# First half of the first layer's W2 from a split operand, two lower parts by accumulating DMAs, and the last store whole on one queue

## The chip, the core and the metric

The kernel runs on one core of one Trainium2 chip. The metric is the device time of one execution in microseconds. A core has a matrix engine (PE, with its weight loads shown as PEld), a vector engine (DVE), a scalar engine (ACT), a general engine (POOL) and a queue engine (SP); each takes its own instructions in program order and waits on semaphores for the others. SP and ACT issue DMAs; in the changed kernel POOL issues two as well.

## The reference

Two layers follow each other on x of shape 4 x 512 x 256, all in float32. Each layer takes a layer norm `xn` of x, a mixer `s` of it, and a feed-forward `g`, and sets `x = x + s * silu(g)`.

- Mixer of layer 0: a recurrence that starts from a zero state, so that only its input part is left: `y = sum over 16 of (C_real*B_real - C_imag*B_imag) * (xn @ W_in.T)`, then `y @ W_out.T`, an RMS norm with weight `norm_w`, and the residual `xn`.
- Mixer of layer 1: a second layer norm with gamma and beta, causal attention with one head of 256, an output projection, and the residual.
- Feed-forward of both layers: `hidden = silu(xn @ W1.T) * (xn @ W3.T)` with 1024 columns, a Walsh-Hadamard transform of `hidden` along the 1024, and `hidden @ W2.T` back to 256 columns.

## The kernel before

**Split operands.** Most float32 operands of PE are kept as a pair of type fp32r: `hi` is the value rounded to fp32r, `lo` is the value less `hi`. A product of two pairs is three products, hi·hi, hi·lo and lo·hi. `split(src, hi, lo)` (L59) makes a pair with two instructions: `nc.scalar.copy` on ACT (L61) rounds, and a `tensor_tensor` subtract on DVE (L62) gives the rest.

**Folded weights.** The Hadamard transform is put into W2 (`prep_w2`, L143): for each half of the 256 output columns, three rounds of adds and subtracts on DVE (`w2b`, L155 and L156) transform across the eight blocks of 128 rows, and a product with the 128 x 128 Sylvester matrix transforms within a block. The result `w2ps` goes through `split` into `w2h` and `w2l`. For the first half of layer 0 the product takes the float32 matrix `had_f` and the float32 `cur` as they are (`native`); for the other three halves `cur` is split into `w2bh` and `w2bl` and multiplied with the fp32r matrix `had` in two products. W_in, W_out and the B, C sums are folded into one 256 x 256 matrix `m` (`prep_m`, L191): `wgh`, `wgl` are W_out scaled by `g`, `wih`, `wil` are W_in split, and `mps` is their product.

**The up weights** `w13` of layer 0 come in four quarters of 512 KB (`load_w13`), each split into hi and lo when the feed-forward first needs it (`split_w13`, L122). They are held in SBUF and used for all four batches.

**Order.** The batch loop runs the feed-forward `ffn` of layer 0 for one batch at a time. For each of its eight column chunks c it emits six products for the gate (`gu` j = 0) and six for the linear part (j = 1), silu on ACT (L527), the gate multiply on DVE (L528), a split of the hidden chunk, and the down products `dn`. The products of `gu` go to three rotating PSUM banks, so that a bank must have been read by silu or by the gate multiply before the third next product can begin. Between the chunks, `Beside` hands out steps of other tasks. In batch 0 the tasks are `prep_first` (L965: the W2 of layer 0, `prep_m`, the load of the next x) and the mixer. A scheduler with a timing model then decides the order on each engine within these dependencies; `after(ins)` asks that what follows is placed behind `ins`. The task steps therefore do not alone decide the order: an engine's order in the built program does. Scratch tiles of `w2b` for layer 0 lie in the slots of later x tiles (`x_slot`), so the loads of x 1 to 3 wait for them.

**The end.** In layer 1 `gate_tile` (L1058) ends the last batch in four tiles of 128 rows: silu on ACT (L1061), multiply (L1063) and add (L1064) on DVE, and a store. Each add is placed behind the one before by `first["last"]`. Tiles 0 to 2 are stored whole (128 KB) by SP; tile 3 is stored as two halves of 64 rows, one by SP, one by ACT.

Of the kernel before, what the change touches and what calls it, by code (L numbers as in the profile page):

```python
# [11 lines left out]
F32 = mybir.dt.float32  # L12
# [3 lines left out]
F32R = mybir.dt.float32r  # L16
# [19 lines left out]
def kernel(ctx: ExitStack, tc: tile.TileContext, a: dict, out: bass.AP):  # L36
# [22 lines left out]
    def split(src, hi, lo, engine=nc.vector):  # L59

        h = nc.scalar.copy(hi, src)  # L61
        return h, engine.tensor_tensor(lo, src, hi.bitcast(F32), ALU.subtract)  # L62

    line = {"fixed": False, "last": None}
# [55 lines left out]
    def split_w13(layer, q, raw):  # L122
        both = wp.tile([P, 2, 2, S], F32R, tag="w13", name=f"w13_{layer}_{q}", bufs=4)
        hi, lo = both[:, 0], both[:, 1]
        if (layer, q) != (0, 0):
            split(raw, hi, lo)
            return hi, lo
        halves = [slice(c * D, (c + 1) * D) for c in range(2)]
        split(*(z[:, :, halves[0]] for z in (raw, hi, lo)))
        next(normed)  # L130
        with after(first["norm"][0]), after(first["norm"][1]):
            hi_, lo_ = split(*(z[:, :, halves[1]] for z in (raw, hi, lo)))
        first["w13"] = hi_, lo_
        return hi, lo
# [8 lines left out]
    def prep_w2(layer, raws, dst, scratch):  # L143

        w2h, w2l = dst
        for half in range(2):
            ds_ = slice(half * P, (half + 1) * P)
            cur = raws[half]  # L150
            for st, h in enumerate((1, 2, 4)):
                nxt = scratch(f"w2b{st}_{layer}_{half}", [P, NH, P])
                cv = cur.rearrange("p (g two h) d -> p g two (h d)", two=2, h=h)
                nv = nxt.rearrange("p (g two h) d -> p g two (h d)", two=2, h=h)
                nc.vector.tensor_tensor(nv[:, :, 0], cv[:, :, 0], cv[:, :, 1], ALU.add)  # L155
                nc.vector.tensor_tensor(nv[:, :, 1], cv[:, :, 0], cv[:, :, 1], ALU.subtract)  # L156
                cur = nxt
                yield

            native = layer == 0 and half == 0  # L160
            if not native:
                bh = t4(f"w2bh_{layer}_{half}", [P, NH, P], F32R)
                bl = t4(f"w2bl_{layer}_{half}", [P, NH, P], F32R)
                split(cur, bh, bl)
                yield
            for q in range(2):
                o = psum(f"w2ps_{layer}_{half}_{q}", [P, NH // 2, P])
                qs = slice(q * NH // 2, (q + 1) * NH // 2)
                if native:
                    matmul(o, had_f, cur[:, qs, :], start=True, stop=True)  # L170
                else:
                    matmul(o, had, bh[:, qs, :], start=True, stop=False)
                    matmul(o, had, bl[:, qs, :], start=False, stop=True)
                split(o, w2h[:, qs, ds_], w2l[:, qs, ds_])
                yield

# [11 lines left out]
        nc.sync.dma_start(win, a["w_in"].rearrange("(c p) i -> p c i", p=P))  # L188
        return win, wout

    def prep_m(win, wout):  # L191

        cb = wp.tile([P, 4, 2, DS], F32, name="cb")
        nc.vector.tensor_tensor(cb, bc[:, :, 0:2, :], bc[:, :, 2:4, :], ALU.mult)
        cbd = wp.tile([P, 4, DS], F32, name="cbd")
        nc.vector.tensor_tensor(cbd, cb[:, :, 0, :], cb[:, :, 1, :], ALU.subtract)
        g = wp.tile([P, 4], F32, name="g")
        nc.vector.tensor_reduce(g, cbd, AX.X, ALU.add)
        wg = [t4(f"wg{i}", [P, 4, D], F32R) for i in "hl"]
        wi = [t4(f"wi{i}", [P, 4, D], F32R) for i in "hl"]  # L200
        for c in range(4):
            nc.scalar.mul(wg[0][:, c, :], wout[:, c, :], g[:, c : c + 1])
            nc.vector.scalar_tensor_tensor(
                wg[1][:, c, :], wout[:, c, :], g[:, c : c + 1], wg[0][:, c, :].bitcast(F32),
                ALU.mult, ALU.subtract,
            )
        split(win, *wi)
        yield
        hi, lo = (wp.tile([P, 2, D], F32R, name=f"m{i}") for i in "hl")
        o = psum("mps", [P, 2, D])  # L210
        for i in range(2):
            mm3(
                o[:, i, :],
                [(tuple(z[:, k, sl(i)] for z in wi), tuple(z[:, k, :] for z in wg)) for k in range(4)],
            )
        split(o, hi, lo)
        first["m"] = hi, lo
        yield
# [247 lines left out]
    def ffn(name, xT, w13, w2, slot, defer=1, spare=(), parts=1, behind=False, tail=()):  # L466
# [34 lines left out]
        for c in range(NH):  # L501
            with after(gates[-2] if behind and c >= 2 else None):
                wh, wl = w13(c // 2)
            gu = []
            for j in range(2):

                o = psum(f"{name}gu{c}_{j}", [P, S], **(DN[0] if behind and c == 1 else GU))
                cols = slice((c % 2) * D + j * P, (c % 2) * D + (j + 1) * P)
                gu.append((o, cols))
            for half in range(parts if c == 0 else 1):  # L510
                n = S // (parts if c == 0 else 1)
                ts_ = slice(half * n, (half + 1) * n)
                if parts == 1 or c:
                    for o, cols in gu:
                        last_up = mm3(o[:, ts_], k_pairs((wh, wl), cols, xT, ts_))
                    continue

                for n, (w, x) in enumerate(((wh, xT[0]), (wl, xT[0]), (wh, xT[1]))):
                    for o, cols in gu:
                        for k in range(2):  # L520
                            last_up = matmul(
                                o[:, ts_], w[:, k, cols], x[:, k, ts_],
                                start=n + k == 0, stop=n + k == 3,
                            )
            gu = [o for o, _ in gu]
            h = hid(f"{name}h{c}")
            first["silu"] = nc.scalar.activation(h, gu[0], AF.Silu)  # L527
            gates.append(nc.vector.tensor_tensor(h, h, gu[1], ALU.mult))  # L528
            first["gate"] = gates[-1]
            if c < len(spare):  # L530
                hh, hl = spare[c]
            else:
                hh = hid(f"{name}hh{c}", F32R)
                hl = hid(f"{name}hl{c}", F32R)
            if c < len(spare):
                nc.scalar.copy(hh, h)
                late.append((hl, h, hh))
            else:
                split(h, hh, hl)
            for _ in range(2 if c >= NH - 2 else 0):  # L540
                if late:
                    lo_, h_, hi_ = late.pop(0)
                    with after(gates[-1]):
                        nc.vector.tensor_tensor(lo_, h_, hi_.bitcast(F32), ALU.subtract)
            queue.append((c, hh, hl))
            ups = last_up if behind else None
            with after(gates[-1] if behind else None), after(ups):
                slot(2 * c)
            if len(queue) > defer:
                down(*queue.pop(0))  # L550
            with after(gates[-1] if behind else None), after(ups):
                slot(2 * c + 1)
# [412 lines left out]
    def prep_first():  # L965
        steps = prep_w2(0, raw2, w2, x_slot)
        with after(first["w13"][1]):
            next(steps)
        yield
        for _ in range(4):  # L970
            next(steps)
            yield
        with after(first["silu"]):
            nc.scalar.copy(had, had_f)
        for _ in range(2):
            next(steps)
            yield
        for _ in range(2):
            next(steps)
            yield  # L980
        load_x(1)
        product = prep_m(*raw_m)
        next(product)
        yield
        next(steps)
        yield
        next(product)
        yield
        yield from steps
# [15 lines left out]
    for b in range(B):  # L1005
        tasks = []
        if b == 0:
            prep = prep_first()
            next(prep)
            tasks.append((prep, 12))  # L1010
        if b:
            tasks.append((call(gate_all, f"g0_{b - 1}", dn, xns[0, b - 1], xs[b - 1]), 1))
        tasks.append((mixer(b), MIXER))
# [44 lines left out]
    def gate_tile(t, o):  # L1058
        x, s = xs[B - 1][:, t, :], xns[1, B - 1][:, t, :]
        g = t2(f"gl{t}", [P, D])  # L1060
        nc.scalar.activation(g, o, AF.Silu)  # L1061
        with after(first.get("last")):
            nc.vector.tensor_tensor(g, g, s, ALU.mult)  # L1063
        first["last"] = nc.vector.tensor_tensor(x, x, g, ALU.add)  # L1064
        if t + 1 < NT:
            nc.sync.dma_start(out[B - 1, sl(t), :], x)
            return

        for queue, rows in ((nc.sync, slice(0, P // 2)), (nc.scalar, slice(P // 2, P))):
            queue.dma_start(out[B - 1, sl(t), :][rows], x[rows])  # L1070

    loaded = {}

# [127 lines left out]
```

## Time and profile before

| what | value |
|---|---|
| median of 3 runs | 359.46 us (359.22 to 359.85) |
| the profiled execution | 359.25 us |
| its span, first to last instruction | 357.5 us |
| PE busy | 350.7 us, 98% of the span |
| DVE busy | 287.2 us, 80% |
| ACT busy | 197.5 us, 55% |
| POOL busy | 20.8 us, 6% |
| granted PE clock | 0.998 |
| DMA | 52.25 MB, mean 146 GB/s |

1.8 us of the execution lie outside the span. Shares of the whole span hide stages: the kernel has a start of some 8 us in which the inputs arrive, a long middle, and an end of some 5 us. The lines of a timeline give start, duration, engine, source line, operation, output <- inputs, shapes and a count of merged instructions; where a line merges several, the time to the next line's start says more than the duration, because products overlap their neighbours. DVE and ACT instructions overlap a little too: a 128x512 subtract shows 0.68 us, and the next starts 0.60 us after it.

### The profile page before, as it was taken

The page shows a single profiled execution, that of the slowest core. Times are in us where ns is not written, and L with a number is a line of the kernel's source. Part 1 is how long each engine was busy: PE and PEld are TensorE (multiplying, and loading weights), DVE is VectorE, ACT ScalarE, POOL GpSimd, SP SyncE. Part 2 cuts the span into 40 slices and gives each one's busy share as a digit, 9 for nine tenths or more (in the row PEclk, how much of TensorE's full clock was granted, in tenths as well). Part 3 has the DMA queues.
Part 4 walks back from the last instruction along what each step waited for, and adds up shares of the span by engine and source line. Part 5 has one row for each costly group of instructions (what it writes and reads, how often), then busy time and mean ns, then how long its engine had stood idle before and what let it go on. Part 6 is the DMA issues. An engine that isn't in the chain of part 4 may idle for free.

```text
span 357.5 us, 6276 instructions
## 1 busy us (share of the span) xinstructions
PE 350.7 (98%) x2477; PEld 326.8 (91%) x2477; DVE 287.2 (80%) x597; ACT 197.5 (55%) x373; POOL 20.8 (6%) x22
## 2 busy tenths in 40 slices
PE   7999999999999999999999999999999999999994
PEld 5878998888988898888999999999999999999994
DVE  6899659998579938998887957989679897577645
ACT  4666166265463425674467745586455676555443
POOL 2000110300021110100100001100011000000000
PEclk9999999999999999999999999999999999999999
DMA  7935000301054316756257135662554635444401
GB/s 241 337 87 211 2 1 2 117 0 61 0 169 174 131 42 230 257 179 200 96 210 261 54 153 208 229 234 73 201 208 172 217 145 205 176 146 173 185 0 59
DMA packets 16300, 52.25 MB, mean 146 GB/s; under 512 B 1648, under 2 KB 7952, under 8 KB 16272
## 3 DMA queue, kind: packets, MB, share of 16 engines
q1 hardware_dynamic: 15904, 51.54, 40.9%
q8 instruction: 19, 0.31, 0.4%
q10 hardware_dynamic: 368, 0.33, 0.3%
q14 instruction: 9, 0.07, 0.1%
HBM read 42.40 MB, written 9.45 MB: 145 GB/s over the span
## 4 chain that ended last, share of the span: by engine, by line
PE 95%; DVE 3%; DMA 1%; ACT 0%; issue 0%; DVEq 0%
PE f_0dn L70 6%; PE f_1dn L70 6%; PE f_2dn L70 6%; PE f_0gu L70 6%; PE f_1gu L70 6%; PE f_2gu L70 6%; PE f_3gu L70 6%; PE f_3dn L70 5%; PE sc L70 4%; PE pv L70 4%; PE o L70 3%; PE v L70 3%; PE tq L70 3%; PE w2ps L70 1%; PE pt L70 1%; PE mps L70 1%
## 5 line engine op out<-in xcount | busy, mean ns | idle before, releaser
L70 PE MATMUL f_3gu<-xt,w 128*128 128x512 f32 x96 | 25.0, 396 | 0.0
L70 PE MATMUL f_2gu<-xt,w 128*128 128x512 f32 x96 | 24.8, 395 | 0.0
L70 PE MATMUL f_1gu<-xt,w 128*128 128x512 f32 x96 | 24.8, 395 | 0.0
L70 PE MATMUL f_0gu<-xt,w 128*128 128x512 f32 (+1 forms) x108 | 24.3, 378 | 0.0
L70 PEld LDWEIGHTS f_0gu<-xt,w 128*128 128x128 f32 x108 | 18.4, 188 | 4.6 <-issue 0.7
L70 PEld LDWEIGHTS f_1gu<-xt,w 128*128 128x128 f32 x96 | 17.0, 188 | 3.1
L70 PEld LDWEIGHTS f_2gu<-xt,w 128*128 128x128 f32 x96 | 17.0, 188 | 3.0
L70 PEld LDWEIGHTS f_3gu<-xt,w 128*128 128x128 f32 x96 | 17.0, 188 | 2.9
L61 ACT CAST f_2hh<-f_2h 128x512 fp32r<-128x512 f32 x16 | 10.0, 622 | 15.5 <-DVE f_2h L528 12.4
L70 PE MATMUL f_3dn<-w2l,f_3hh 128*128 128x256 f32 x64 | 17.7, 281 | 0.0
L70 PE MATMUL f_3dn<-w2h,f_3hh 128*128 128x256 f32 x64 | 17.7, 281 | 0.0
L70 PE MATMUL f_1dn<-w2l,f_1hh 128*128 128x256 f32 x64 | 17.7, 281 | 0.0
L70 PE MATMUL f_2dn<-w2h,f_2hh 128*128 128x256 f32 x64 | 17.7, 282 | 0.0
L70 PE MATMUL f_1dn<-w2h,f_1hh 128*128 128x256 f32 x64 | 17.6, 280 | 0.0
L70 PE MATMUL f_2dn<-w2l,f_2hh 128*128 128x256 f32 x64 | 17.6, 281 | 0.0
L70 PE MATMUL f_3dn<-w2h,f_3hl 128*128 128x256 f32 x64 | 17.0, 281 | 0.0
L70 PE MATMUL f_1dn<-w2h,f_1hl 128*128 128x256 f32 x64 | 17.0, 281 | 0.0
L70 PE MATMUL f_2dn<-w2h,f_2hl 128*128 128x256 f32 x64 | 16.7, 281 | 0.0
L61 ACT CAST f_3hh<-f_3h 128x512 fp32r<-128x512 f32 (+1 forms) x17 | 10.0, 594 | 10.1 <-DVE f_3h L528 5.9
L61 ACT CAST f_1hh<-f_1h 128x512 fp32r<-128x512 f32 x16 | 9.9, 622 | 9.7 <-DVE f_1h L528 6.6
L62 DVE TENSOR_TENSOR f_2hl<-f_2h,f_2hh 128x512 fp32r<-128x512 f32 x16 | 10.9, 684 | 4.5 <-ACT f_2hh L61 4.5
L62 DVE TENSOR_TENSOR f_3hl<-f_3h,f_3hh 128x512 fp32r<-128x512 f32 (+1 forms) x17 | 11.0, 654 | 3.7 <-ACT f_3hh L61 3.6
(487 smaller groups left out, 1145.9 us busy)
## 6 DMA issues: line engine op xcount, KB each, us to landing
sw<-s SPq DMA_DIRECT2D x32, 896.0 KB, 5.2
s<-sp SPq DMA_DIRECT2D x8, 512.0 KB, 4.3
s<-sp SPq DMA_DIRECT2D x8, 384.0 KB, 2.8
w2raw<-in_w SPq DMA_DIRECT2D x4, 512.0 KB, 5.6
sraw<-in_w SPq DMA_DIRECT2D x4, 512.0 KB, 3.6
mrb<-there SPq DMA_DIRECT2D x4, 512.0 KB, 3.7
w13raw<-in_w SPq DMA_DIRECT2D x3, 512.0 KB, 7.1
x<-in_x SPq DMA_DIRECT2D x3, 512.0 KB, 3.6
```

Source lines behind the costliest of these rows:

```text
L61: h = nc.scalar.copy(hi, src)
L62: return h, engine.tensor_tensor(lo, src, hi.bitcast(F32), ALU.subtract)
L70: ins = call(*args, **kwargs)
```

## The change

- In `prep_w2` the `native` path goes: the first half of layer 0 is split into `w2bh` and `w2bl` and multiplied with `had` in two products per quarter, as the other three halves are.
- A new helper `split_by_dma` makes a pair without DVE: ACT writes `-src`, rounded to fp32r, into `lo`; ACT copies `src` rounded into `hi`; and POOL issues a DMA that adds `src` onto `lo`. Quarter 3 of the up weights and W_in are made this way. The former is placed behind the third silu of batch 0.
- The split of W_in moves from `prep_m` into `prep_first`, before the second half of W2, and `prep_first` is counted as 13 steps instead of 12.
- In `gate_tile` the last tile is stored whole by SP, and only the adds of tiles 2 and 3 are entered in `first["last"]`.

```diff
+    def split_by_dma(src, hi, lo):
+        nc.scalar.mul(lo, src, -1.0)
+        nc.scalar.copy(hi, src)
+        nc.gpsimd.dma_start(lo.bitcast(F32), src, accum_op=ALU.add)
...
-        if (layer, q) != (0, 0):
-            split(raw, hi, lo)
+        if q:
+            with after(first["silus"][2] if q == 3 else None):
+                (split_by_dma if q == 3 else split)(raw, hi, lo)
             return hi, lo
...
-            native = layer == 0 and half == 0
-            if not native:
-                bh = t4(f"w2bh_{layer}_{half}", [P, NH, P], F32R)
-                bl = t4(f"w2bl_{layer}_{half}", [P, NH, P], F32R)
-                split(cur, bh, bl)
-                yield
+            bh = t4(f"w2bh_{layer}_{half}", [P, NH, P], F32R)
+            bl = t4(f"w2bl_{layer}_{half}", [P, NH, P], F32R)
+            split(cur, bh, bl)
+            yield
...
-                if native:
-                    matmul(o, had_f, cur[:, qs, :], start=True, stop=True)
-                else:
-                    matmul(o, had, bh[:, qs, :], start=True, stop=False)
-                    matmul(o, had, bl[:, qs, :], start=False, stop=True)
+                matmul(o, had, bh[:, qs, :], start=True, stop=False)
+                matmul(o, had, bl[:, qs, :], start=False, stop=True)
...
-    def prep_m(win, wout):
+    def prep_m(wi, wout):
...
-        wi = [t4(f"wi{i}", [P, 4, D], F32R) for i in "hl"]
...
-        split(win, *wi)
...
             first["silu"] = nc.scalar.activation(h, gu[0], AF.Silu)
+            first.setdefault("silus", []).append(first["silu"])
...
-        for _ in range(4):
+        for _ in range(3):
             next(steps)
             yield
         with after(first["silu"]):
             nc.scalar.copy(had, had_f)
         for _ in range(2):
             next(steps)
             yield
-        for _ in range(2):
+        win, wout = raw_m
+        wi = [t4(f"wi{i}", [P, 4, D], F32R) for i in "hl"]
+        split_by_dma(win, *wi)
+        for _ in range(4):
             next(steps)
             yield
         load_x(1)
-        product = prep_m(*raw_m)
+        product = prep_m(wi, wout)
...
-            tasks.append((prep, 12))
+            tasks.append((prep, 13))
...
-        first["last"] = nc.vector.tensor_tensor(x, x, g, ALU.add)
-        if t + 1 < NT:
-            nc.sync.dma_start(out[B - 1, sl(t), :], x)
-            return
-
-        for queue, rows in ((nc.sync, slice(0, P // 2)), (nc.scalar, slice(P // 2, P))):
-            queue.dma_start(out[B - 1, sl(t), :][rows], x[rows])
+        ins = nc.vector.tensor_tensor(x, x, g, ALU.add)
+        if t > 1:
+            first["last"] = ins
+        nc.sync.dma_start(out[B - 1, sl(t), :], x)
```

## The prediction

> **What bounds the kernel now.** I read the page first, then the chain of waits, then the stretches in which the change lies, engine by engine.
>
> ```profile
> PE 350.7 (98%) x2477; PEld 326.8 (91%) x2477; DVE 287.2 (80%) x597; ACT 197.5 (55%) x373; POOL 20.8 (6%) x22
> PE 95%; DVE 3%; DMA 1%; ACT 0%; issue 0%; DVEq 0%
> 20.00:31.00 11.00, 11.00 (x47) 8.54 (x46) 11.00 (x21) 7.51 (x14) 0.00 (x0) 1.00 0.49 147
> 51.00:75.00 24.00, 24.00 (x140) 20.91 (x140) 23.11 (x47) 11.06 (x25) 3.42 (x2) 1.00 0.13 44
> ```
>
> The second line is the chain by engine; the last two are windows (length, then PE, PEld, DVE, ACT, POOL busy, clock, DMA share, GB/s). From 8 to 352 us PE is the path without a hole, at the full clock. So a product saved there is time saved, and a wait put there is time lost. DVE is as full as PE in 20 to 31 us and nearly so in 51 to 75, so its order decides whether PE's banks come free in time. Next, the chain in order of time (start, length, what), for the products that change:
>
> ```profile
> 17.87 0.86 PE w2ps L70 x2
> 18.73 1.40 PE f_0gu L70 x6
> 20.13 0.86 PE w2ps L70 x2
> 27.29 0.23 PE w2ps L70
> ```
>
> One native float32 product takes PE 0.86 us, one product of the split kind 0.23, and six up products 1.40. Then the end, from the timelines of DVE, SP and ACT (start, length):
>
> ```profile
> 353.89 0.42 DVE L1064 TENSOR_TENSOR x<-x,gl 128x256 f32<-128x256 f32 x1
> 354.34 0.55 SPq L1070 DMA_DIRECT2D out<-x  x1
> 354.35 0.57 ACTq L1070 DMA_DIRECT2D out<-x  x1
> out<-x SPq DMA_DIRECT2D x1, 64.0 KB, 2.0
> out<-x ACTq DMA_DIRECT2D x1, 64.0 KB, 2.3
> ```
>
> The last two, from the DMA view, say how long the halves take to land; after the later one 0.8 us of closing waits remain to 357.5.
>
> **The change part by part.**
>
> W2's first half. Two native products (2 x 0.86) become four split ones (4 x 0.23): 0.80 us less on PE, all on the path. The new split costs ACT one 1024-wide copy (1.05 us) and DVE one 1024-wide subtract, from which the next instruction starts 1.14 later.
>
> The two lower parts. DVE loses two 1.14 us subtracts (rows of w13's last quarter, 25.33, and of `wil`, 30.51). ACT gains two 1024-wide multiplies; the trace has none, so I take its 512-wide activation and cast (0.59 and 0.62) as equal and give each the 1024 cast's 1.05, starting the next 0.95 later. Both copies move earlier.
>
> The waits that this makes, walked along the new orders of the engines with row durations, and 0.05 us from one engine's end to another's start. To 17.71 nothing changes for PE.
> - ACT: the third silu needs the second `early` copy, which needs the gate multiply that ends at 16.13, so silu runs at 16.69, the multiply for `lo` at 17.18, its copy at 18.12, and the new `w2bh` only at 19.06, to 20.11. PE has done six up products by 19.11 and three more by 19.81, and its next are the two `w2bh` products: a wait of 0.35.
> - DVE: the third gate begins at 17.32; then the first `w2b` pair of the second half to 19.12, w13's third quarter to 20.26, the next pair to 21.46, the new `w2bl` to 22.60, and the fourth gate ends at 23.28. PE arrives at the chunk that needs that bank at 23.20 and goes on at 23.33: a wait of 0.13.
> - From there I find no late partner until the up products of batch 0 are done: gates at 25.28 and 29.09 against PE at 26.13 and 30.34, `w2bh` of the second half at 25.98 against 27.53. PE reaches the point that was at 36.06 at 35.74.
> - So 0.80 - 0.48 = 0.32 us are left. The cover of these waits is ACT's spare time; with ACT free earlier they would be nothing, and with each ACT step 0.1 us longer the first would be 0.6.
>
> Batch 1's order moves too: DVE does the whole first `w2b` chain before the second gate. The first gate starts 4.12 us after batch 1's first product (when its silu is done). Up to the fourth gate DVE has six `w2b` pairs (12 x 0.60), three gates and three lower parts (6 x 0.60), the norm's statistics (1.78), `w2bl` (1.13), the scaled mixer rows (1.59) and the residual (1.13): 16.43. With the gate's own 0.68 and the handover it is done at 21.28 after that first product, and PE wants the bank at 21.16. A wait of 0.12; the sum is good to about 0.3, so the bounds are nothing and 0.5. Net so far 0.20. Everything behind has DVE holes in the trace before, and I put it at nothing, within 0.3 either way.
>
> The adding DMAs. Neither a DMA issued by POOL nor an accumulating one is in the trace. Nearest rows: 512 KB loads land 3.1 us (`qkraw`) to 8.9 us (w13's last quarter, in the crowded start) after issue; the x loads, alone, 3.6; 896 KB takes 5.2. An add reads its target as well, so about 1 MB of reads, and on from 3.6 and 5.2 that is some 5.7: my value, since the DMA engines idle at 19 to 21.5 us; bounds 3.1 to 8.9. The first is issued at 18.2, and PE, which would stand before three waiting products, wants it at 26.8: 8.6 us of cover. The second is issued at 22.1, beside the loads of x 1 and 2, and is wanted at 31.9: 9.8 us. So both cost nothing by the value, 0.3 by the upper end. The scale of W_out on DVE also waits for the first (slot), at 28.9. Behind them on POOL stands the power of batch 1's norm at 40, long after. The x loads on SP keep their releases (the second half's `w2b` at 21.5, 24.7, 27.9) within 0.1.
>
> POOL's own work shows a price beside a full DVE: the same 128x4 power takes 1.01 us at 40.66 and 1.91 at 64.71. If POOL's part in a DMA is stretched alike, that is inside my bounds. The Trainium skill, SBUF — State Buffer, "Summary: rules for kernel authors", speaks against the change: it says not to hide a POOL-issued DMA under DVE work, because its descriptors starve; "Who interferes with whom" limits that to DVE's two-port modes, which it says `tensor_tensor`, all that DVE runs at 18 to 24 us, does not have. By the strict rule the first add would start only when DVE runs dry, some us after PE stops at 26.8, and the sum would turn to a loss of several us, an estimate; by the limit it is as above. DMA: Bandwidth & Descriptors, "Anatomy of one DMA", gives 2.0 us plus bytes at 436 GB/s, an estimate of 3.2 us for a plain 512 KB; by it the sum stays.
>
> The end. Each add no longer follows the one before for tiles 0 and 1, so DVE runs gl, gl, x, x without a dependent pair: the last add ends 0.08 earlier (pairs show 0.45, independent ones 0.35). The halves land at 356.36 and 356.64, 2.0 and 2.3 after issue. The trace's landing counts put the three whole 128 KB stores just before at 1.70 to 1.72 after theirs. The fourth, issued in the same rhythm, I give 1.70: 0.60 less. Bounds: 1.70, and 2.29 if the halves' lateness has nothing to do with being two.
>
> **Sum.** 0.20 + 0.08 + 0.60 = 0.88 us. The profiled execution has 359.25, so 358.37; it lies 0.21 below the median of the runs, to which this belongs: 358.6.
>
> **The rivals.**
> 1. The adding DMA is late. POOL prepares it slowly beside a full DVE, or the add runs far below a copy's rate. PE stands at the second three products of chunk 6; each us beyond 8.6 is 1 us lost. The gain is gone at 9.5 us and it is measurably slower from 10.2. At 11 us: 358.6 + 2.4 = 361.0. For it: no row to hold it back, and the 1.91 us power. Against: idle DMA engines, and twice the loads' 3.6 is still in time.
> 2. The gain is eaten by waits: ACT's four 1024-wide steps in a row, or batch 1's DVE order, cost 0.6 more than walked, or the whole store lands like the halves. 359.2.
> 3. It does less harm than walked: PE meets no wait, since a scheduler placed it so; 0.6 more: 358.0.
>
> **How the numbers follow.** Forecast 0.55 (own range 358.1 to 359.0), rival 1 0.16, rival 2 0.21, rival 3 0.08. A measurement here can tell about 0.2%, 0.72 us, so faster means under 358.74. Of the forecast 0.44 lies below that; with rival 3 and 0.03 of rival 2, 0.55. Slower: rival 1 beyond 360.18, 0.13. The rest, 0.32, is the same. The range goes from 357.8 (rival 3 and the spread of the runs) to 360.4, which leaves out most of rival 1 and little else.
>
> **What would show it.** In the profile after: four `w2ps` products of 0.23 for half 0; PE holes of about 0.3 before the first and 0.1 before chunk 5; no PE wait for a POOL DMA; the store landing 1.7 after issue; the last add 0.2 to 0.3 earlier. A PE wait at chunk 6 of a us or more, or an end within 0.2 us of the old one, would make it wrong.

## The result, and the profile after

The changed kernel takes 360.41 us (median of ten runs, 360.15 to 360.82), the kernel before 359.44 us on the same chip. The ratio is 1.0029, with a 95% interval of 1.0021 to 1.0038: slower by about 1.0 us, where 358.6 and faster was forecast. The profiled execution took 360.69 us with a span of 358.9, at a granted clock of 1.00 throughout. Of the kernels further down, one execution of e5_no_dma (699 us) and one of e8_three (381 us) were in a slow state and are not in the medians given.

The same lines of the page as before, PE's busy time and the chain by engine:

```profile
PE 352.0 (98%) x2477; PEld 327.4 (91%) x2477; DVE 286.5 (80%) x596; ACT 200.3 (56%) x376; POOL 22.8 (6%) x24
...
PE 85%; DVE 10%; ACT 2%; DMA 2%; issue 1%; SPq 0%; DVEq 0%; ACTq 0%
```

The chain was 95% PE; now 15% of it runs through other engines. PE is being waited for less, and waits more. The two stretches as before (length, then PE, PEld, DVE, ACT, POOL busy, clock, DMA share, GB/s):

```profile
20.00:31.00 11.00, 10.97 (x49) 8.34 (x48) 11.00 (x21) 10.00 (x19) 0.86 (x1) 1.00 0.90 213
51.00:75.00 24.00, 23.74 (x135) 20.38 (x134) 22.07 (x44) 10.53 (x24) 4.73 (x2) 1.00 0.14 44
```

In the first, ACT has gone from 7.51 to 10.00 us busy and the DMA engines from 0.49 to 0.90; PE is still full. In the second PE has lost 0.26 us and runs five products fewer in the same time. The products that change, from the chain in order of time:

```profile
16.81 3.50 PE f_0gu L76 x15
20.34 0.74 PE w2ps L76 x2
...
23.17 0.60 PE w2ps L76 x2
...
28.10 0.23 PE w2ps L76
```

Two pairs of split products stand where two native ones took 0.86 each. The 0.74 and 0.60 for two products of 0.23 hold waits, and a product's modelled end beside them. From the starts, the first pair has 0.19 in front of it and 0.11 within it, the second 0.03 and 0.11. The DMA view (KB each, us from issue to landing), for the adding DMAs, the x loads beside them and the last stores:

```profile
x<-in_x SPq DMA_DIRECT2D x3, 512.0 KB, 7.1
...
w<-w13raw POOLq DMA_DIRECT2D x1, 512.0 KB, 5.2
wil<-win POOLq DMA_DIRECT2D x1, 512.0 KB, 6.5
...
out<-x SPq DMA_DIRECT2D x4, 128.0 KB, 1.7
```

The adds are done in 5.2 and 6.5 us, in time for PE; the three x loads beside the second one land 7.1, 6.5 and 5.1 us after issue (the view's 7.1 is the first) instead of 3.5 to 3.7, and no engine waits for them. The four stores of the last tiles land after 1.7 to 1.8 us. So far the change does what it was to do. What it lost is in another view, the waits of PE behind the start (who waits for whom, us in total, times, longest):

```profile
PE f_3dn L76 <- DVE f_3hl L62: 0.6, 1, 0.6
PE f_1gu L76 <- DVE f_1h L528: 0.3, 1, 0.3
PE f_2dn L76 <- DVE f_2hl L62: 0.2, 1, 0.2
```

There was no such line before. This view counts from the modelled end of a product, so it gives too little. Start to start, against the 0.234 and 0.119 us that products of 512 and 256 columns otherwise need, the three holes, stretches that PE loses, are 0.53 us at 72.0 (batch 1), 0.49 at 113.6 (batch 2) and 0.83 at 170.6 (batch 3), 1.85 together. In each, 0.10 of it lies behind the wait: the product that ends the wait is followed 0.10 late as well.

None of the three lies where the diff edits the code. They come, as the experiments show, from the new order in which the scheduler put the instructions of batches 1 to 3. The first, from the timeline (start, length):

```profile
71.19 0.69 DVE L163 TENSOR_TENSOR w2b<-w2b 128x512 f32<-128x512 f32 x1
...
71.79 0.68 DVE L528 TENSOR_TENSOR f_1h<-f_1h,f_1gu 128x512 f32<-128x512 f32 x1
...
72.53 0.96 PE L76 MATMUL f_1gu<-xt,w 128*128 128x512 f32 x3 [0.26 <-DVE f_1h L528]
```

The gate multiply of chunk 3 stands behind a `w2b` pair; its silu was done at 68.8, and PE needed the bank at 72.1. The second:

```profile
109.35 0.84 ACT L61 CAST sp<-sraw 128x768 fp32r<-128x768 f32 x1 [3.58 <-DMA sraw<-in_w]
110.09 0.61 ACT L61 CAST f_2hh<-f_2h 128x512 fp32r<-128x512 f32 x1
...
112.53 0.92 DVE L62 TENSOR_TENSOR sp<-sraw,sp 128x768 fp32r<-128x768 f32 x1
...
113.53 0.66 DVE L62 TENSOR_TENSOR f_2hl<-f_2h,f_2hh 128x512 fp32r<-128x512 f32 x1
...
114.24 0.38 PE L76 MATMUL f_2dn<-w2h,f_2hl 128*128 128x256 f32 x1 [0.23 <-DVE f_2hl L62]
```

ACT stands 3.58 us before the cast of a transferred tile with the cast that PE's chain needs behind it, and DVE takes that tile's `sp` ahead of `f_2hl`. The third, from the chain in order of time:

```profile
158.09 0.32 SPq L352
...
158.50 5.49 DMA sraw<-in_w
...
164.11 0.42 DVE ssum L332
...
166.15 0.87 DVE sp L62
167.02 0.60 DVE f_3h L528
...
168.93 1.12 DVE sp L62
170.05 0.60 DVE tql L62
...
170.81 0.59 DVE f_3hl L62
...
171.44 0.62 PE f_3dn L76 x3
```

L352 is the second load of the first `sw` pair. It waits for PE to release its slot until 158.07, and the load of `sraw` for the last `prep_s` (L327) stands behind it on SP. In the kernel before, `sraw` is issued at 148.39 between the two `sw` loads (timeline of SP):

```profile
148.02 0.32 SPq L353 DMA_DIRECT2D sw<-s  x1
148.39 0.43 SPq L328 DMA_DIRECT2D sraw<-in_w  x1
155.92 0.32 SPq L353 DMA_DIRECT2D sw<-s  x1
```

Ten us later than there, it makes DVE's queue late to the end of the layer.

At the first product of layer 1 the changed kernel is 2.06 us behind before's trace (0.32 of it from its very first up product on), and from there nothing changes until the end gives back 0.64.

### The profile page after: what moved, and what is told of

It reads as the page before. It is cut to its first block, busy times and chain, and to the rows that moved or that the text cites. A ratio compares the mean times of both kernels' runs of the same rounds, so it can differ in the third digit from the quotient of the medians.

```text
span 358.9 us, 6288 instructions
## 1 busy us (share of the span) xinstructions
PE 352.0 (98%) x2477; PEld 327.4 (91%) x2477; DVE 286.5 (80%) x596; ACT 200.3 (56%) x376; POOL 22.8 (6%) x24
## 4 chain that ended last, share of the span: by engine, by line
PE 85%; DVE 10%; ACT 2%; DMA 2%; issue 1%; SPq 0%; DVEq 0%; ACTq 0%
PE f_0dn L76 6%; PE f_0gu L76 6%; PE f_2dn L76 5%; PE f_1dn L76 5%; PE f_3dn L76 5%; PE f_3gu L76 5%; PE sc L76 4%; PE pv L76 4%; PE f_1gu L76 3%; PE v L76 3%; PE f_2gu L76 3%; PE tq L76 2%; PE o L76 2%; PE warm L76 2%; DMA sraw<-in_w 2%; DVE sp L62 1%
```

## The experiments

My theory from the trace: the edited parts bring what I forecast, and the loss is the order behind them. Main rival: the adding DMAs cost the time, by traffic or on POOL. Several kernels below hold an engine's order: a chain of order-only edges, appended behind the traced program, puts the instructions of each engine in a given sequence and changes nothing else.

```diff
+    traced = nc.cur_bb.bb.instructions[start_:]
+    for text in order_.values():
+        prev = None
...
+                if prev is not None:
+                    tc.add_manual_dep(traced[k], prev.name, mybir.DependencyInfo(
+                        mybir.DependencyClass.NoSync, mybir.DependencyReason.DATA), reason="order")
+                prev = traced[k]
```

**The end alone** (e1_end): before, with the new `gate_tile`.

```diff
-        first["last"] = nc.vector.tensor_tensor(x, x, g, ALU.add)
-        if t + 1 < NT:
-            nc.sync.dma_start(out[B - 1, sl(t), :], x)
-            return
...
+        ins = nc.vector.tensor_tensor(x, x, g, ALU.add)
+        if t > 1:
+            first["last"] = ins
+        nc.sync.dma_start(out[B - 1, sl(t), :], x)
```

> The kernel before with only the end of the change: the last tile stored whole by SP, only the adds of tiles 2 and 3 chained. Every engine's order ahead of the last tiles is that of before. My theory (the end brings what I forecast, the loss is elsewhere): the last store lands 1.70 us after issue, the last add is 0.08 earlier, 358.8 us against 359.44 (ratio 0.9981 to 0.9985). Rival (the end's gain in the changed kernel was run spread or came from its other timing): 359.4, ratio 1.000.

Measured: 358.60 against 359.23 us, ratio 0.9982 [0.9973, 0.9991]. From PE's last product to the last add it is 0.10 shorter than before, from there to the end of the span 0.60. The end is worth what was forecast, 0.65 us.

**The changed kernel in the old order** (e2_old_order): `order_` holds, from batch 1 on, the order of the kernel before.

> The changed kernel, whole, with both adding DMAs, but from batch 1 on each engine is held to the order that it had in the kernel before; batch 0 and the end are the changed kernel's own. My theory (what is lost are three waits that come from the new order of DVE, ACT and SP behind batch 0: 0.52 at chunk 3 of batch 1, 0.49 in batch 2, 0.84 in batch 3): batch 0's gain of 0.22 and the end's 0.64 are left, 358.6 us, ratio 0.9976. Rival 1 (the adding DMAs and the transfers that they slow cost the time, whatever the order): it stays at 360.4, ratio 1.003. Rival 2 (the first x loads land 0.3 later whenever POOL issues DMAs): first up product 0.3 later than before, 358.9.

Measured: 358.38 us, ratio 0.9979 [0.9970, 0.9987]. Its page and its second stretch:

```profile
PE 350.5 (98%) x2477; PEld 327.0 (92%) x2477; DVE 286.3 (80%) x596; ACT 200.2 (56%) x376; POOL 22.7 (6%) x24
...
PE 98%; DVE 1%; ACT 0%; issue 0%
...
51.00:75.00 24.00, 24.00 (x141) 20.94 (x140) 21.45 (x45) 10.95 (x25) 3.42 (x2) 1.00 0.13 44
```

Both adding DMAs are in it (5.3 and 6.5 us), so is the split, and the chain is PE again; 51 to 75 is full. The ratio is 0.0050 below the changed kernel's, 1.80 us, and the three holes make 1.85. Rival 1 is out. Its first up product is at 7.47 us, earlier than before's 7.80, so the later start of the changed kernel's trace does not follow whenever POOL issues DMAs.

**The old kernel in the new order** (e3_new_order): before, unedited but for `order_`, which holds the changed kernel's order from batch 1 on.

> The reverse: the kernel before, with its own batch 0 and its own end and no adding DMA, but from batch 1 on held to the order of the changed kernel. My theory: it pays the three waits, up to 0.52 + 0.49 + 0.84 = 1.85 us, less where its batch 0 ends with other spare time: 360.9 to 361.4, ratio 1.004 to 1.0055. Rival 1 (the adding DMAs cost the time): 359.4, ratio 1.000.

Measured: 360.89 us, ratio 1.0049 [1.0035, 1.0063]. PE's waits are at the same three places:

```profile
PE f_1gu L70 <- DVE f_1h L528: 0.3, 1, 0.3
PE f_2dn L70 <- DVE f_2hl L62: 0.2, 1, 0.2
PE f_3dn L70 <- DVE f_3hl L62: 0.2, 1, 0.2
```

The third is smaller, 0.48 from start to start instead of 0.83. The 1.66 us lost lie at the lower end of what I expected. So the order costs some 0.5% with the old batch 0 as with the new one, without a single edited instruction and without an adding DMA.

**One transfer moved** (e4_sraw): the changed kernel, PE, DVE, ACT and POOL held to its own order, and

```diff
-        nc.sync.dma_start(raw, a["w13_1"][q])
+        first["sraw"] = nc.sync.dma_start(raw, a["w13_1"][q])
...
-            nc.sync.dma_start(parts[i].bitcast(F32), sdram[q][i])
+            with after(first["sraw"] if n == 0 and i == 1 else None):
+                nc.sync.dma_start(parts[i].bitcast(F32), sdram[q][i])
```

> The changed kernel with one transfer moved: the load of sraw of the fourth prep_s stands on SP ahead of the second load of sw instead of behind it, as in the kernel before; all other engines are held to the changed kernel's order. My theory (this load, issued 10 us late behind a DMA that waits for PE, made DVE late for f_3hl and PE late by 0.84 us): the wait of PE at 170.6 is gone, 359.6 us, ratio to before 1.0004. Rival (DVE in batch 3 is too full anyway, the load only shows where it stops): half of the wait stays or more, 360.0 to 360.4.

Measured: 359.54 us, ratio 1.0008 [0.9999, 1.0017]. The hole in batch 3 is gone, the other two are as before it (0.53 and 0.49). One DMA on another place of one queue is worth 0.8 us.

**The other two waits, one at a time** (e6_gate, e7_hl), all engines held to the changed kernel's order but for the moves:

```diff
 DVE, e6_gate
+f_1h (gate of chunk 3, batch 1)
 w2b2_1_1 (add)
 w2b2_1_1 (subtract)
-f_1h (gate of chunk 3, batch 1)
 ACT, e7_hl
+f_2hh (chunk 2)
 sp<-sraw
-f_2hh (chunk 2)
 DVE, e7_hl
+f_2hl (chunk 2)
 ssum (first)
...
-f_2hl (chunk 2)
```

> The changed kernel with every engine's whole order as it is, and one instruction moved: on DVE the gate multiply of chunk 3 of batch 1 stands ahead of the last w2b pair instead of behind it. My theory (PE's hole of 0.52 us at 72.0 is the bank that this multiply frees 0.5 late): the hole is gone and nothing takes its place, 0.5 less than the changed kernel, 359.9 us, ratio to before 1.0015. Rival (the w2b chain that is now 0.6 later, or a later wait, takes it back): 360.4, ratio 1.003.

Measured: 359.79 us, ratio 1.0012 [1.0003, 1.0020]. The hole is gone, and PE is 0.51 earlier relative to its entry into batch 1: as expected.

> The changed kernel with every engine's whole order as it is, and two instructions moved: on ACT the cast f_2hh of chunk 2 stands ahead of the cast sp<-sraw that waits 3.6 us for a transfer, and on DVE f_2hl of that chunk stands ahead of ssum. My theory: PE's hole of 0.49 us at 113.6 is gone, 359.9 us, ratio 1.0015. Rival (the waits behind, in batch 3, grow by as much, since the same DVE work is only done later): 360.4, ratio 1.003.

Measured: 360.19 us, ratio 1.0027 [1.0018, 1.0036]. A miss. The hole of 0.49 is gone, but another of 0.28 opens 1 us later (timeline of DVE and PEld):

```profile
112.89 0.93 DVE L62 TENSOR_TENSOR sp<-sraw,sp 128x768 fp32r<-128x768 f32 x1
...
114.02 0.66 DVE L528 TENSOR_TENSOR f_2h<-f_2h,f_2gu 128x512 f32<-128x512 f32 x1
...
114.73 1.22 PEld L76 LDWEIGHTS f_2gu<-xt,w 128*128 128x128 f32 x6 [0.23 <-DVE f_2h L528]
```

The work of `prep_s` that I moved behind `f_2hl` is now in front of the next gate, which frees a bank. My theory named the wait that came first and not the next in DVE's queue: 0.21 of 0.49 was won there, and 0.11 in batch 3.

**All four instructions** (e8_three): the moves of e4, e6 and e7 in one kernel.

> All the moves together: the gate multiply of chunk 3 of batch 1, the two instructions of chunk 2 of batch 2, and the load of sraw on SP ahead of the second load of sw. Four instructions of the changed kernel stand elsewhere, nothing else. My theory (the three waits are independent and are all that the changed kernel lost): 0.52 + 0.49 + 0.83 less, 358.5 us, ratio 0.9975, the same as with the whole order of before. Rival (other parts of the new order cost too, or the waits are linked): 359.0 to 359.6, ratio 0.999 to 1.0005.

Measured: 358.84 us, ratio 0.9986 [0.9977, 0.9995]. Between theory and rival: 1.55 us less than the changed kernel, 0.25 short of the old order. That is about the size of e7's new wait of 0.28; that it is this wait is not shown. Four instructions out of some six thousand turn the changed kernel from slower to faster.

**Without the adding DMAs** (e5_no_dma, and e12_no_dma_again for its trace), from batch 1 on in the old order:

```diff
     def split_by_dma(src, hi, lo):
-        nc.scalar.mul(lo, src, -1.0)
-        nc.scalar.copy(hi, src)
-        nc.gpsimd.dma_start(lo.bitcast(F32), src, accum_op=ALU.add)
+        split(src, hi, lo)
```

> The changed kernel without the adding DMAs: quarter 3 of the up weights and W_in are split by ACT and DVE (two more 1.14 us subtracts on DVE in batch 0), W2's first half still from a split operand; from batch 1 on the order of the kernel before, as in the run that held that order with both adding DMAs (358.38 us). My theory (the adding DMAs are hidden and their worth is DVE's time in batch 0, where DVE has no idle time from 16 to 36 us): some of 2.3 us of DVE work comes through to PE, 358.8 to 359.6 us, ratio 0.999 to 1.001. Rival 1 (the adding DMAs cost time by their traffic): faster than 358.38. A third view (DVE's extra work is hidden by order, the DMAs are worth nothing): 358.3 to 358.5.

> The kernel with the split and without the adding DMAs again, for its trace: it lost 2.4 us against the one with them. My theory: in batch 0 PE stands 2 to 2.5 us in waits for DVE (gates, w2bl and the lower part of quarter 3), between 20 and 50 us; from batch 1 on it is as with the DMAs. Rival: the loss is behind batch 0, because the order held there fits another batch 0.

Measured: 360.96 us, ratio 1.0046 [1.0032, 1.0060], and 360.89 in the execution of e12; PE's waits behind the start, and the stretch 16 to 36 us of this kernel and of the one with the DMAs:

```profile
PE f_0gu L72 <- DVE f_0h L524: 0.9, 1, 0.9
PE mps L72 <- DVE wgl L199: 0.9, 1, 0.9
...
16.00:36.00 20.00, 18.16 (x79) 13.77 (x78) 20.00 (x35) 14.22 (x25) 0.00 (x0) 1.00 0.43 134
```

```profile
16.00:36.00 20.00, 19.98 (x99) 16.06 (x99) 19.79 (x39) 16.14 (x27) 1.91 (x2) 1.00 0.75 205
```

I had expected part of DVE's 2.3 us to come through; 2.4 us did, as much as all of it. DVE has 20.00 of 20 us busy, PE stands 0.31 and 1.26 before gates and 1.06 with 0.4 of late products behind it before `wgl`, and up to its entry into batch 1 it has lost 2.84 us against the trace with the DMAs (whose execution, 358.07, lies 0.31 below its median); behind that no more than 0.05. Batch 0 was held neither here nor in e2, so its order differs too: the 2.4 us are the price of the two subtracts in the order that the scheduler then chose, and another order was not tried. The x loads land 3.3 to 4.3 us after issue here instead of 5.1 to 7.0, and that brings nothing.

**Native products with the adding DMAs** (e9_native_dma), from batch 1 on in the old order:

```diff
+            native = layer == 0 and half == 0
+            if not native:
+                bh = t4(f"w2bh_{layer}_{half}", [P, NH, P], F32R)
...
+                if native:
+                    matmul(o, had_f, cur[:, qs, :], start=True, stop=True)
```

> W2's first half from the native float32 operand as before, but with both adding DMAs and the end of the changed kernel; from batch 1 on the order of the kernel before. It fills the fourth corner beside native without the DMAs (the end alone, 0.9982), split without them (1.0046) and split with them (0.9979). My theory (PE had no hole in batch 0 before, so DVE's 2.3 us less work is worth nothing by itself; the DMAs pay only for the split's new DVE work): the same as the end alone, ratio 0.998, 358.6 to 358.8 us. Rival (the relief on DVE and ACT gains by itself, or the DMAs' traffic costs by itself): 0.3 us or more to either side of that.

Measured: 358.68 us, ratio 0.9982 [0.9973, 0.9991], the same as the end alone. So of the four corners, all with the new end: native 0.9982 without and 0.9982 with the DMAs, split 1.0046 without and 0.9979 with them. The DMAs are worth 2.4 us to the split and nothing to the native form.

**A better order in batch 0** (e10_best): e2 with two moves (the second `w2b` pair goes along with the first, on which it depends).

```diff
 ACT
+w2bh_0_0
 w13_0_3 (multiply)
 w13_0_3 (copy)
-w2bh_0_0
 DVE
-w2b0_0_1 (add, subtract)
 w13_0_2 (subtract)
-w2b1_0_1 (add, subtract)
 w2bl_0_0
 f_0h (gate of chunk 3)
+w2b0_0_1 (add, subtract)
+w2b1_0_1 (add, subtract)
```

> The changed kernel with the order of before from batch 1 on, and in batch 0 two moves: on ACT w2bh ahead of the multiply and the copy of quarter 3, on DVE the first w2b pair of the second half behind w2bl and the gate multiply of chunk 3. My theory (batch 0 still holds the waits that I walked, 0.29 for w2bh on ACT and 0.3 for w2bl and the gate on DVE; they come from order, not from work): all of them gone, 0.5 to 0.6 less than without the two moves, 357.9 us, ratio 0.9965. Rival (what is moved back is late next: the second half's w2bh, or the loads of x that wait for w2b): 358.4 or more, ratio 0.998 or more.

Measured: 358.31 us, ratio 0.9973 [0.9962, 0.9983], the lowest of all, faster than before and than the changed kernel. The waits at 19.5, 22.4 and 23.0 are gone; a new one of 0.31 opens at 25.5, where PE waits for a gate multiply, so only half of the gain that I expected is kept. By the interval it is not told from e2.

**The first adding DMA held back** (e11_late): e2, with one POOL instruction that waits for `w2bl`.

```diff
         nc.scalar.copy(hi, src)
+        if "extra" not in first:
+            late = small("late")
+            ins = nc.gpsimd.tensor_tensor(late, first["w2bl"][:, 0, :NT].bitcast(F32), mhalf, ALU.mult)
...
-        nc.gpsimd.dma_start(lo.bitcast(F32), src, accum_op=ALU.add)
+        with after(first["late"]):
+            nc.gpsimd.dma_start(lo.bitcast(F32), src, accum_op=ALU.add)
```

> The changed kernel with the order of before from batch 1 on, and the first adding DMA held back: POOL first runs a 128x4 multiply that reads w2bl of the first half, so that the DMA is issued at about 23 us instead of 18.1. This measures its cover. My theory (the cover is real and sharp): landing at 28.3 to 28.8 against PE's first need at 26.65, so 1.7 to 2.1 us on the path, 360.1 to 360.6 us, ratio 1.002 to 1.0035. Rival (PE has other work to pull in, or the DMA had been waiting for something else anyway): under 0.5 us, 358.4 to 358.9.

Measured: 361.83 us, ratio 1.0072 [1.0050, 1.0095]; the single runs are 360.93, 361.02, 362.64 and 363.00. More than the theory's 2.1 at most. The DMA is issued at 23.41 and lands at 29.48, after 6.07 us; PE stands 2.45 us beyond a product's time. Its wait, and three stretches behind it:

```profile
PE f_0gu L81 <- DMA w<-w13raw: 2.3, 1, 2.3
...
30.00:31.00 1.00, 1.00 (x6) 0.80 (x5) 1.00 (x4) 0.00 (x0) 0.00 (x0) 0.99 1.21 248
31.00:32.00 1.00, 1.00 (x4) 0.76 (x3) 0.40 (x1) 0.00 (x0) 0.00 (x0) 0.50 1.03 166
...
35.00:36.00 1.00, 1.00 (x6) 0.81 (x5) 1.00 (x2) 0.84 (x2) 0.00 (x0) 1.00 1.03 389
```

The cover of the DMA is real and ends where it was worked out. In the profiled execution (362.64) the wait costs more than its length, since the granted clock falls to 0.50 from 31.0 to 34.4 us. The mean granted clocks of the four runs are 1.000 and 0.999 for the pair at 361.0, 0.992 and 0.995 for the other: by the ratios to before, the faster pair lost 2.4 us against e2, the wait and no more.

## Why the prediction was wrong, step by step

- **W2's first half, right in kind, 0.1 too good in size.** The saving of 0.80 and the waits of 0.35 and 0.13 gave 0.32 net. The traces have 0.29 before `w2bh`, as walked, 0.14 to 0.15 at `w2bl`, a wait that I had not walked, and 0.13 at the gate of chunk 3: 0.57 in all, which leaves 0.23. From the first up product to batch 1 five traces with the new batch 0 take 42.96 us on average; of those with the old one, before takes 43.14 and e3 43.21, so the gain is 0.22. (e1, also with the old one, takes 43.48, but its trace has a wait of 0.27 at 15.6, ahead of the products that change, that the other two do not have.) In the medians (0.9979 against 0.9982) only 0.1 of it is seen, and by the intervals even that is not told from nothing.
- **The adding DMAs, right.** Value 5.7 us, measured 5.2 and 6.5; no wait. Rival 1 had no place in this kernel. Its point at 8.6 us of cover is confirmed by e11; its slope of 1 us for each us beyond holds in two of e11's four runs, and the other two lost 1.8 us more. What I did not see is how much hung on the DMAs: 2.4 us. I had put DVE's saved subtracts beside the new one and never priced the change without them. The Trainium skill, SBUF — State Buffer, "Summary: rules for kernel authors", advises against a POOL-issued DMA under a DVE instruction because its descriptors starve while DVE is in its 2x or 4x mode; my "strict rule" left this condition out. With DVE busy in `tensor_tensor` all through 20 to 24 us, the add landed 5.2 us after issue, inside the range of plain loads, so nothing of the kind shows here.
- **The end, right.** 0.68 forecast, 0.70 in e1's trace, 0.65 in its median.
- **Batch 1, mis-sized.** The place was right, the gate multiply of chunk 3 behind the `w2b` chain. Counted from batch 1's first product the gate was done at 21.43 (forecast 21.28) and PE was there at 21.06 (forecast 21.16), and the restart, which I had not counted, adds 0.10: 0.53 in place of 0.12, just beyond the upper bound of 0.5.
- **"Everything behind has DVE holes in the trace before, and I put it at nothing, within 0.3 either way": the step that failed.** It cost 1.3 us: 0.49 in batch 2 and 0.83 in batch 3. DVE does have holes there, but I read them off a trace whose order the changed kernel no longer had. I walked the new orders of ACT and DVE up to batch 1 and stopped, and never read SP's, where the reversed pair of loads stood in plain sight. A load that waits for PE to release its slot holds up the loads behind it: here `sraw` until 158.50, and moving it ahead of that load gave back 0.8 us (e4).
- **The rivals.** Rival 2, "the gain is eaten by waits", comes nearest; it named batch 1's DVE order, but priced the whole at 0.6 and stopped at "same". No rival had waits beyond batch 1, so nothing on the slower side stood for what happened. The signs that the prediction named lie in batch 0 and at the end, and the loss lies between: only the last add, forecast 0.2 to 0.3 us earlier and measured 1.98 later (356.29 against 354.31), tells of it.

With the order of before held, the kernel does 0.9979. That order has no wait in batch 1, so the terms that bear on it are 0.32 + 0.08 + 0.60 = 1.00 us, or 0.9972: inside the interval (0.9970 to 0.9987) and about 0.25 us more than was measured. The sum of the edited parts was near, and it was the sum of a kernel that was not built. That the forecast's own 0.88, or 0.9976, comes closer still is luck: it takes off a wait that this kernel does not have.

What stays open: the traces with adding DMAs put the first up product at 7.47 to 8.12 us (eight, mean 7.86), those without at 7.40 to 7.80 (four, mean 7.57). Whether POOL's DMAs delay the start by some 0.2 us or this is the spread of the first loads, these runs don't tell; it would explain why the medians show less of batch 0's gain than the traces. Nor was it tried why the scheduler chose the order that it did.

## What to carry to other kernels

Where a scheduler decides the order, an edit is priced in two parts: what the edited instructions cost, and what the new order of everything behind them costs. Read the second off the built program, every engine and every DMA queue down to the end, and look for an instruction that waits long (a load for a slot, a cast for a transfer) in front of one that PE needs. To tell the two parts apart, hold the old order in the new kernel and the new order in the old one; here that took two runs, and four moved instructions then gave back most of the loss.

## What the runs showed of the hardware

- A wait of PE costs 0.10 us more than its length: behind each wait read here the product that follows takes 0.34 instead of 0.23 us (0.22 instead of 0.12 for 256 columns).
- Behind a wait of 2.45 us the clock went down, in some executions. In e11's trace products of 512 columns start 0.43 us apart from 31.0 to 34.4, at a granted clock of 0.50 for 3.41 us, 1.5 us after PE had started again; that costs some 1.5 us. The two pairs of its runs (361.0 and 362.8) lie 1.8 apart. The Trainium skill, TensorE: Matmul & The Clock Gate, "Part 1: The HAM clock gate (the "warmup" mystery)", has the half clock follow at least one idle window of about 3.4 us; here less sufficed in that execution, and waits of 0.3 to 1.3 us in the other traces left the clock at 1.00.
- A 512 KB accumulating DMA from SBUF to SBUF, issued by POOL, took 5.2 to 7.3 us (7.3 for the second one in e9), and 9.8 us for the second one in e11, which ran beside the first; POOL was held for 0.86 to 1.2 us by each. In the changed kernel three 512 KB loads beside them took 5.1 to 7.1 us instead of 3.5 to 3.7.
- A whole 128 KB store by one queue landed 1.7 us after issue (1.8 for the second of the four in the changed kernel), where its halves by two queues took 2.0 and 2.3.
